# A graph-network kernel: the edges in eight parts in place of seven, the last part smaller and packed three tiles to two blocks

## The chip, the cores and the metric

One core of one Trainium2 chip runs one program. The metric is the device time of an execution in microseconds (us). A core has five engines that run their own instruction streams in order and wait for each other through semaphores: TensorE (PE; its weight loads are listed apart as PEld), VectorE (DVE), ScalarE (ACT), GpSimd (POOL) and SyncE (SP, which here only issues DMAs).

## The reference, cut to what matters

There are 6250 nodes and 100000 edges with 128 features each; the edges are sorted by `dst`.

```python
row, col = src, dst
h   = concat([x[row], x[col], edge_attr]) @ W + b      # 384 -> 128, one row per edge
h   = layernorm(h) * gamma + beta
msg = relu(h)
out = segment_sum(msg, row, 6250)                       # summed by source node
x   = layernorm(x + out)
```

## The kernel before

The edges come as 782 tiles of 128, sorted by destination, and the sum goes by source. So the kernel sorts the edges by source on the way. Source nodes are cut into 50 **blocks** of 125 nodes, and two neighbouring blocks make a **pair**, 25 pairs in all. The edges are cut into seven **splits** (table `SPLITS`: tiles in the split, tiles of room for each block, rows of a block that are always filled, and sizes of the pieces in which places are computed).

*The loop over pieces.* A piece `q` is four tiles, 196 pieces in all. For each, PE multiplies the edge features with their part of `W` (L620) and adds the destination's part by a one-hot matmul (L624, 126 of 128 rows used); DVE builds that one-hot (L608, `ohd`); ACT evicts the result to one of nine buffers `hs` (L634); and POOL scatters each tile's rows, one indirect DMA a tile (L651), to `sorted_d[s]` in DRAM, where every pair of blocks has its own region. The rows of the pair's two blocks alternate there. A scatter is tied by a semaphore to PE's progress in the same piece (`scatters`), and an eviction waits until the scatters of the buffer's earlier content are done. DVE, PE and ACT also compute the places (`places`).

*Old pairs.* When a split's scatters are done, its pairs can be worked off (class `Pairs`). A pair is loaded back (`load_pairs`, `hl`), a tile of 128 rows at a time: one-hots of the source nodes `ohe` (DVE, L749), their transposes (PE L761, ACT L765), a copy of the rows to PSUM (ACT L771), the source part added by three bf16 matmuls a tile (`pick`, PE L788), squares and their root (ACT L797, L800), the scaled and cut message (DVE L806, L812), the sum over edges by an f32 one-hot matmul (`sums`, PE L821, into the bank `pa`) and the addition to `acc` (DVE L827). Two pairs of four tiles go as one item of eight (a *twin*), where the code says so; the rest are single items. An item takes four steps, written in the table `FLOW`; `steps_due(q)` says how many steps must stand in the program by piece `q`. It is a straight line between marks: the pairs of split `s - 1` begin at the piece in which split `s` begins plus `LAG` = 5, and those of the last split but one must be over at piece 197.

*The tail.* The last split's pairs are worked off behind the last scatter (class `Unit`, function `tail`): a unit of one pair, eleven of two, and two of one. A unit does what `Pairs` does (loads L848, one-hots L855, transposes L865, copy to ACT or by an f32 identity matmul on PE L877, picks L888, squares L899, messages L914, sums L928, addition L934) and then the final layer norm (L941 to L984, partly on POOL). PE, DVE, ACT and SP run in the order in which the code is written.

*Names in the views.* `sel`, `hp`, `pa`, `tr` and `beside` are PSUM banks. L552 is a check, run once: a matmul with a single column of weights (`ones_f`).

## Time and profile before

| | us |
|---|---|
| three runs: median, lowest, highest | 1112.56, 1111.35, 1113.34 |
| the profiled execution, its own time | 1110.36 |
| its span, first to last instruction | 1108.6 |

| engine | PE | PEld | DVE | ACT | POOL |
|---|---|---|---|---|---|
| busy, us of the span | 865.3 | 799.1 | 858.5 | 767.3 | 796.4 |

A row of a timeline gives an instruction's start, its duration, engine, line, operation and tiles, and in brackets how long the engine sat idle before it and what ended that. A row that merges several ("x8") gives the stretch that they took. An instruction's duration reaches beyond the start of the next, since they are pipelined; what an instruction costs its engine is read from start to start. A row of windows gives a stretch and the busy time and count (x) of an engine in it.

### The profile page before, as it was taken

How to read it: one execution, taken by the hardware profiler on the slowest of the kernel's cores; microseconds unless marked ns; L12 is line 12 of the kernel's file. 1: busy time of each engine (PE TensorE's matmuls, PEld its weight loads, DVE VectorE, ACT ScalarE, POOL GpSimd, SP SyncE). 2: the span in 40 equal slices, each digit the busy share in tenths (PEclk: the TensorE clock that was granted, in tenths of full speed). 3: DMA queues.
4: the chain of work that ended last, by engine and by line, in shares of the span. 5: the costliest groups of instructions: out<-in, count | busy, mean ns of one | idle time of the engine just before them, and what ended most of it. 6: DMA issues, size and time to landing. Idle time of an engine off the chain costs nothing. (4 is left out here: it accounts for less than half of the span.)

```text
span 1108.6 us, 27458 instructions
## 1 busy us (share of the span) xinstructions
PE 865.3 (78%) x8878; PEld 799.1 (72%) x8878; DVE 858.5 (77%) x2436; ACT 767.3 (69%) x3049; POOL 796.4 (72%) x830
## 2 busy tenths in 40 slices
PE   6758656456989898698868868788889788885994
PEld 4647545446889788688768868678888788875773
DVE  8874656636898997869687777889898977764997
ACT  4324422126889888588676778798889787976896
POOL 2777777777777777777777777777777777775254
PEclk9878887668999999889899989999999999998998
DMA  6899999648877888777587767686789777833341
GB/s 212 246 279 270 278 316 296 217 161 273 285 249 233 256 250 261 240 222 226 165 263 235 250 196 237 210 291 204 223 250 292 239 215 210 245 115 117 117 132 64
DMA packets 132851, 250.59 MB, mean 226 GB/s; under 512 B 47805, under 2 KB 62031, under 8 KB 132697
## 3 DMA queue, kind: packets, MB, share of 16 engines
q1 hardware_dynamic: 106724, 195.30, 59.0%
q0 software_dynamic: 25104, 53.05, 13.4%
q8 instruction: 71, 1.16, 0.5%
q14 instruction: 82, 0.67, 0.2%
q10 hardware_dynamic: 870, 0.40, 0.1%
HBM read 155.49 MB, written 93.18 MB: 224 GB/s over the span
## 5 line engine op out<-in xcount | busy, mean ns | idle before, releaser
L651 POOL DMA_INDIRECT sorted<-hs,place_i x782 | 758.1, 969 | 243.3 <-issue 96.6
L821 PE MATMUL pa<-msg,ohe 128*128 128x130 f32 x1700 | 237.1, 288 | 30.8 <-DVE acc L827 22.8
L788 PE MATMUL sel<-xa,ohn 128*128 128x128 bf16 x2550 | 190.9, 224 | 83.2 <-ACT sel L771 82.5
L620 PEld LDWEIGHTS hp<-w,eT 128*128 128x128 f32 x1564 | 216.7, 213 | 49.8 <-issue 29.2
L620 PE MATMUL hp<-w,eT 128*128 128x128 f32 x1564 | 238.5, 301 | 16.7 <-ACT hs L634 16.7
L797 ACT ACTIVATE sq<-sel 128x128 f32<-128x128 f32 x850 | 224.0, 279 | 39.2 <-PE sel L788 37.7
L812 DVE SCALAR_TENSOR_TENSOR msg<-sel,rstd,cut 128x128 f32<-128x128 f32 x850 | 243.0, 345 | 8.8
L821 PEld LDWEIGHTS pa<-msg,ohe 128*128 128x128 f32 x1700 | 211.0, 197 | 38.9 <-DVE acc L827 26.2
L788 PEld LDWEIGHTS <-ohn 128*128 128x128 bf16 x2550 | 165.0, 100 | 93.8 <-issue 85.4
L797 ACT ACTIVATION_READ_ACCUMULATOR sq<-sel 128x1 f32 x850 | 178.8, 210 | 0.0
L749 DVE TENSOR_TENSOR ohe<-hl,beside 128x768 f32<-128x768 f32 (+2 forms) x130 | 132.2, 1017 | 36.8 <-PE beside L503 21.3
L634 ACT COPY hs<-hp 128x512 f32<-128x512 f32 x196 | 113.1, 579 | 50.3 <-PE hp L624 47.6
L771 ACT COPY sel<-hl 128x384 f32<-128x384 f32 (+1 forms) x250 | 132.1, 529 | 19.9 <-DVE msg L812 19.2
L765 ACT COPY ohn<-tr 128x768 bf16<-128x768 bf16 (+2 forms) x130 | 109.6, 843 | 5.9 <-PE tr L761 5.9
L608 DVE TENSOR_SCALAR ohd<-db,part_w 128x512 bf16<-128x512 bf16 x192 | 69.6, 363 | 56.5 <-DMA db<-drel_d 31.0
L827 DVE TENSOR_TENSOR acc<-acc,pa 128x260 f32<-128x260 f32 x150 | 62.8, 419 | 51.9 <-PE pa L821 51.6
L569 ACT COPY hs<-sloc 128x12 f32<-128x12 f32 x66 | 14.1, 214 | 112.6 <-DMA sorted<-hs,place_i 110.8
L624 PE MATMUL hp<-win,ohd 126*128 126x128 bf16 x782 | 81.7, 230 | 1.7 <-DMA win<-xb_d 1.7
L761 PE MATMUL tr<-ident_h,ohe 128*128 128x128 bf16 x850 | 70.8, 223 | 13.3 <-issue 10.4
L800 ACT ACTIVATE std<-ss,eps 128x3 f32<-128x3 f32 (+1 forms) x250 | 74.2, 297 | 8.1
L806 DVE RECIPROCAL rstd<-std 128x3 f32<-128x3 f32 (+1 forms) x250 | 42.3, 169 | 46.7 <-ACT std L800 44.5
L624 PEld LDWEIGHTS <-ohd 126*128 126x128 bf16 x782 | 65.8, 104 | 5.4 <-issue 2.0
(200 smaller groups left out, 1033.0 us busy)
## 6 DMA issues: line engine op xcount, KB each, us to landing
eT<-in_eT SPq DMA_DIRECT2D x96, 512.0 KB
hl<-sorted SPq DMA_DIRECT2D x75, 396.0 KB
db<-drel_d SPq DMA_DIRECT2D x96, 256.0 KB
sorted<-empty SPq DMA_DIRECT2D x100, 198.0 KB
hl<-sorted SPq DMA_DIRECT2D x75, 264.0 KB
hl<-sorted SPq DMA_DIRECT2D x25, 528.0 KB
sorted<-hs,place_i POOLq DMA_INDIRECT x782
sorted<-empty SPq DMA_DIRECT2D x75, 132.0 KB
```

Source lines behind the costliest of these rows:

```text
L620: pe(nc.tensor.matmul(hp[:, j, :], eT[:, at], w[:, 2, :], start=j == 0, stop=False, skip_group_check=True), 4)
L624: pe(nc.tensor.matmul(hp[:, j, :], oh[:3 * WN, at], win[:3 * WN, :], start=False, stop=j == m - 1, skip_group_check=True))
L634: nc.scalar.copy(hs[:, :m, 0:D], hp[:, :m, :])
L651: i = nc.gpsimd.indirect_dma_start(out=sorted_d[s][:, :], out_offset=bass.IndirectOffsetOnAxis(ap=place_i[:parts, t:t + 1], axis=0), in_=h ...
L749: nc.vector.tensor_tensor(self.ohe[:, :k, :], self.hl[:, :k, D:D + 1].to_broadcast([P, k, P]), row_bc(iota_p, k), op=ALU.is_equal)
L765: nc.scalar.copy(self.ohn[:, :self.k, :], self.tr[:, :self.k, :])
L771: nc.scalar.copy(self.sel[g][:, :m, :], self.hl[:, j0:j0 + m, 0:D])
L788: pe(nc.tensor.matmul(sel[:, j, :], self.ohn[:, j0 + j, :], xa[:, b, i * D:(i + 1) * D], start=False, stop=j == m - 1 and i == 2, skip_gro ...
L797: nc.scalar.activation(sq[:, j, :], self.sel[g][:, j, :], AF.Square, accum_out=ss[:, j:j + 1])
L800: nc.scalar.activation(std[:, :m], ss[:, :m], AF.Sqrt, bias=eps, scale=1.0 / D)
L812: nc.vector.scalar_tensor_tensor(self.msg[:, j0 + j, 0:D], self.sel[g][:, j, :], rstd[:, j:j + 1], cut, op0=ALU.mult, op1=ALU.max)
L821: pe(nc.tensor.matmul(self.pa[:, h, :], self.ohe[:, i * k + j, :], self.msg[:, i * k + j, :], start=(j == h), stop=(j == k - 2 + h)), 4)
```

## The change

The table has eight splits: the first and two of 124 tiles stand as before, then three of 80, one of 68, and the last of 58 tiles with 1.5 tiles of room for each block. So a pair of the last split has three tiles: one for each block, and a third whose first 64 rows belong to the first block and whose last 64 to the second (`shares`). The third tile is loaded by two DMAs of 64 partitions; in `pick` and `sums` each of its halves gets matmuls of its own, with 64 columns (L905) or 64 rows (L946) of weights. The sums of a unit go to two banks by block and not by pair, and two additions follow with a stride over the pairs. Old pairs are 900 tiles where they were 850, the tail's pairs 75 tiles where they were 100. The first one-hot of the tail is written two steps later among the old pairs' steps.

```diff
-          (124, 3, 192, [42, 42, 40]),
           (80, 2, 128, [40, 40]),
           (80, 2, 128, [40, 40]),
-          (82, 2, 128, [42, 40])]
+          (80, 2, 128, [40, 40]),
+          (68, 2, 128, [34, 34]),
+          (58, 1.5, 96, [30, 28])]
...
+def pair_rows(s):
+    return int(2 * SPLITS[s][1]) * P
+
+def shares(kp, j):
+    if j % 2 == 0 and j == kp - 1:
+        return [(h, slice(h * P // 2, (h + 1) * P // 2)) for h in range(2)]
+    return [(j % 2, slice(0, P))]
...
+    def load_rows(s, p, rows):
+        k, at = pair_rows(s) // P, p * pair_rows(s) * ROW
+        m = k // 2 * 2
+        nc.sync.dma_start(flat(rows[:, :m, :]),
+                          dram_ap(sorted_d[s], at, [[m * ROW, P], [1, m * ROW]]))
+        if m < k:
+            for h, c in shares(k, m):
+                nc.sync.dma_start(rows[c, m, :],
+                                  dram_ap(sorted_d[s], at + (m * P + h) * ROW,
+                                          [[2 * ROW, P // 2], [1, ROW]]))
...
     class Unit:
...
             for j in range(m):
-                b = 2 * (self.p0 + g) + j % 2
-                for i in range(3):
-                    nc.tensor.matmul(sel[:, j, :], self.ohn[:, j0 + j, :],
-                                     xa[:, b, i * D:(i + 1) * D], start=False,
-                                     stop=j == m - 1 and i == 2, skip_group_check=True)
+                for h, c in shares(m, j):
+                    for i in range(3):
+                        nc.tensor.matmul(sel[c, j, :], self.ohn[:, j0 + j, c],
+                                         xa[:, 2 * (self.p0 + g) + h, i * D:(i + 1) * D],
+                                         start=False, stop=j == m - 1 and i == 2,
+                                         skip_group_check=True)
...
         def sums(self, g):
-            if (self.p0 + g) % 2:
-                pa_t = psum.tile([P, PT, P], F32, name="hp", bufs=BANKS["hp"])
-                pa = flat(pa_t)
-            else:
-                pa = psum.tile([P, 512], F32, name="pa")
-            pa = pa[:, :2 * ACW].rearrange("p (h d) -> p h d", h=2)
+            if g == 0:
+                one = psum.tile([P, 512], F32, name="pa")
+                two = flat(psum.tile([P, PT, P], F32, name="hp", bufs=BANKS["hp"]))
+                self.pa = [t[:, :self.n * ACW].rearrange("p (g d) -> p g d", g=self.n)
+                           for t in (one, two)]
             for h in range(2):
-                for j in range(h, self.kp, 2):
+                parts = [(j, c) for j in range(self.kp) for i, c in shares(self.kp, j) if i == h]
+                for j, c in parts:
                     jj = g * self.kp + j
-                    nc.tensor.matmul(pa[:, h, :], self.ohe[:, jj, :], self.msg[:, jj, :],
-                                     start=(j == h), stop=(j == self.kp - 2 + h))
-            self.pa = {**getattr(self, "pa", {}), g: pa}
+                    nc.tensor.matmul(self.pa[h][:, g, :], self.ohe[c, jj, :], self.msg[c, jj, :],
+                                     start=(j == h), stop=(j == parts[-1][0]))
...
     work(n_tail - n_steps)
     for i in range(3):
         units[i].load()
-    work(1)
+    work(3)
     units[0].ones()
...
     units[0].square()
-    work(5)
+    work(n_tail + 11 - n_steps)
```

Three places show how the order moves. The first is DVE between the destination one-hots (`ohd`) of pieces 189 and 190, late in the loop. Before:

```order
L608 TENSOR_SCALAR ohd<-db,part_w 128x512
L749 TENSOR_TENSOR ohe<-hl,beside 128x1024
L806 RECIPROCAL rstd<-std 128x4
L812 SCALAR_TENSOR_TENSOR msg_2205<-sel,rstd,cut 128x128 x4
L827 TENSOR_TENSOR acc<-acc,pa 128x260
L608 TENSOR_SCALAR ohd<-db,part_w 128x512
```

The same place in the changed kernel (its lines are L619, L766, L824, L830, L846):

```order
L619 TENSOR_SCALAR ohd<-db,part_w 128x512
L846 TENSOR_TENSOR acc<-acc,pa 128x260
L824 RECIPROCAL rstd<-std 128x4
L830 SCALAR_TENSOR_TENSOR msg_2209<-sel,rstd,cut 128x128 x4
L766 TENSOR_TENSOR ohe<-hl,beside 128x1024
L824 RECIPROCAL rstd<-std 128x4
L830 SCALAR_TENSOR_TENSOR msg_2208<-sel,rstd,cut 128x128 x4
L846 TENSOR_TENSOR acc<-acc,pa 128x260 x2
L824 RECIPROCAL rstd<-std 128x4
L830 SCALAR_TENSOR_TENSOR msg_2208<-sel,rstd,cut 128x128 x4
L619 TENSOR_SCALAR ohd<-db,part_w 128x512
```

Three message groups of old pairs stand between the two pieces where one stood.

The second place is DVE where the tail begins; L855 (changed: L872) is the first one-hot of the tail, which needs rows of the last split. Before:

```order
L812 SCALAR_TENSOR_TENSOR msg_2205<-sel,rstd,cut 128x128 x4
L855 TENSOR_TENSOR ohe<-hl,beside 128x512
L827 TENSOR_TENSOR acc<-acc,pa 128x260
L806 RECIPROCAL rstd<-std 128x4
L812 SCALAR_TENSOR_TENSOR msg_2204<-sel,rstd,cut 128x128 x4
L855 TENSOR_TENSOR ohe<-hl,beside 128x1024
L827 TENSOR_TENSOR acc<-acc,pa 128x260
L806 RECIPROCAL rstd<-std 128x4
L812 SCALAR_TENSOR_TENSOR msg_2205<-sel,rstd,cut 128x128 x4
L827 TENSOR_TENSOR acc<-acc,pa 128x260
L855 TENSOR_TENSOR ohe<-hl,beside 128x1024
```

In the changed kernel:

```order
L830 SCALAR_TENSOR_TENSOR msg_2209<-sel,rstd,cut 128x128 x4
L872 TENSOR_TENSOR ohe<-hl,beside 128x384
L846 TENSOR_TENSOR acc<-acc,pa 128x260
L824 RECIPROCAL rstd<-std 128x4
L830 SCALAR_TENSOR_TENSOR msg_2208<-sel,rstd,cut 128x128 x4
L872 TENSOR_TENSOR ohe<-hl,beside 128x768
L846 TENSOR_TENSOR acc<-acc,pa 128x260
L872 TENSOR_TENSOR ohe<-hl,beside 128x768
```

Behind the tail's first one-hot stand three additions and two message groups of old pairs before, two and one now.

The third place is PE inside the tail, where the sums of a unit end and the next unit's copy and picks begin. Before, after the transposes:

```order
L865 MATMUL tr<-ident_h,ohe 128x128
L928 MATMUL hp<-msg_2204,ohe 128x130 x4
L928 MATMUL pa<-msg_2204,ohe 128x130 x4
L877 MATMUL hp<-hl,ident 128x512
L888 LDWEIGHTS ohn
L888 MATMUL hp<-xa,ohn 128x128
```

In the changed kernel (of each "x2" the second matmul has 64 rows of weights):

```order
L882 MATMUL tr<-ident_h,ohe 128x128
L946 MATMUL pa<-msg_2209,ohe 128x130 x2
L946 MATMUL hp<-msg_2209,ohe 128x130 x2
L946 MATMUL pa<-msg_2209,ohe 128x130 x2
L946 MATMUL hp<-msg_2209,ohe 128x130 x2
L894 MATMUL hp<-hl,ident 128x384
L905 LDWEIGHTS ohn
L905 MATMUL hp<-xa,ohn 128x128
```

As many matmuls stand there as before, eight, in an order of banks that alternates by block, and the copy is 384 wide in place of 512.

More of the change, by code (lines that the diff above doesn't have):

```diff
@@ L679, in open_late @@
             nc.tensor.matmul(flat(sel), ones_h, row_bc(ones_h, PT), start=True, stop=True)
-    KMAX = 2 * max(k for _, k, _, _ in SPLITS)
+    KMAX = int(2 * max(k for _, k, _, _ in SPLITS))
     MS = 2
@@ L785, in pick @@
             for j in range(m):
-                b = self.block(j0 + j)
-                for i in range(3):
-                    pe(nc.tensor.matmul(sel[:, j, :], self.ohn[:, j0 + j, :],
-                                        xa[:, b, i * D:(i + 1) * D], start=False,
-                                        stop=j == m - 1 and i == 2, skip_group_check=True))
+                p, jj = self.p + (j0 + j) // self.kp, (j0 + j) % self.kp
+                for h, c in shares(self.kp, jj):
+                    for i in range(3):
+                        pe(nc.tensor.matmul(sel[c, j, :], self.ohn[:, j0 + j, c],
+                                            xa[:, 2 * p + h, i * D:(i + 1) * D], start=False,
+                                            stop=j == m - 1 and i == 2, skip_group_check=True))
         def square(self, g):
@@ L819, in sums @@
             for h in range(2):
-                for j in range(h, k, 2):
-                    pe(nc.tensor.matmul(self.pa[:, h, :], self.ohe[:, i * k + j, :],
-                                        self.msg[:, i * k + j, :],
-                                        start=(j == h), stop=(j == k - 2 + h)), 4)
+                parts = [(j, c) for j in range(k) for g, c in shares(k, j) if g == h]
+                for j, c in parts:
+                    pe(nc.tensor.matmul(self.pa[:, h, :], self.ohe[c, i * k + j, :],
+                                        self.msg[c, i * k + j, :],
+                                        start=(j == h), stop=(j == parts[-1][0])), 4)
         def add(self, i=0):
@@ L1241, in tail @@
                 u(-1).sums(g)
-                u(-1).add(g)
+            for h in range(2):
+                u(-1).add(h)
             u(-1).begin(nc.gpsimd)
```

41 lines of the change are left out of this document (18 added, 23 removed).

## Prediction

> **What bounds the kernel now.** I read the page's slices and groups first, then POOL, then the last 100 us engine by engine.
>
> ```profile
> POOL 2777777777777777777777777777777777775254
> ```
> ```profile
> L651 POOL DMA_INDIRECT sorted<-hs,place_i x782 | 758.1, 969 | 243.3 <-issue 96.6
> ```
>
> POOL is equally busy from the second slice to the 36th: 782 scatters of 969 ns with 243.3 us of gaps between them, so one each 1.28 us and 1001 us in all, without a longer stop. Up to the last scatter POOL sets the time. DVE shows what follows it:
>
> ```profile
> 1012.75 1.13 DVE L812 SCALAR_TENSOR_TENSOR msg<-sel,rstd,cut 128x128 f32<-128x128 f32 x4
> 1022.11 0.69 DVE L855 TENSOR_TENSOR ohe<-hl,beside 128x512 f32<-128x512 f32 x1 [8.23 <-DMA hl<-sorted]
> 1022.72 0.42 DVE L827 TENSOR_TENSOR acc<-acc,pa 128x260 f32<-128x260 f32 x1
> 1023.05 0.17 DVE L806 RECIPROCAL rstd<-std 128x4 f32<-128x4 f32 x1
> 1023.25 1.13 DVE L812 SCALAR_TENSOR_TENSOR msg<-sel,rstd,cut 128x128 f32<-128x128 f32 x4
> ```
> ```profile
> 1017.30 0.87 POOL L651 DMA_INDIRECT sorted<-hs,place_i  x1 [0.30 <-issue]
> ```
>
> The old pairs' work is written up to 1014, then DVE sits 8.23 us until rows of the last split are back: the last scatter ends at 1018.2, and its rows are in SBUF 3.9 us later. Then the tail of 100 tiles runs. In its middle a unit of two pairs (eight tiles) looks so:
>
> ```profile
> 1057.07:1062.55 5.48, 5.48 (x56) 4.18 (x53) 5.41 (x24) 5.21 (x29) 3.26 (x4) 1.00 0.45 148
> ```
> ```profile
> 1057.07 1.11 PE L928 MATMUL hp<-msg,ohe 128*128 128x130 f32 x8
> 1058.02 1.06 PE L928 MATMUL pa<-msg,ohe 128*128 128x130 f32 x8
> 1058.91 1.02 PE L877 MATMUL sel<-hl,ident 128*128 128x512 f32 x2
> 1059.84 0.84 PE L888 MATMUL sel<-xa,ohn 128*128 128x128 bf16 x12
> 1060.52 1.08 PE L877 MATMUL sel<-hl,ident 128*128 128x512 f32 x2
> 1061.43 0.83 PE L888 MATMUL sel<-xa,ohn 128*128 128x128 bf16 x12
> 1062.10 0.61 PE L865 MATMUL tr<-ident_h,ohe 128*128 128x128 bf16 x8
> 1062.55 1.11 PE L928 MATMUL hp<-msg,ohe 128*128 128x130 f32 x8
> ```
> ```profile
> 1055.73 2.16 DVE L914 SCALAR_TENSOR_TENSOR msg<-sel,rstd,cut 128x128 f32<-128x128 f32 x8
> 1057.80 1.21 DVE L855 TENSOR_TENSOR ohe<-hl,beside 128x1024 f32<-128x1024 f32 x1
> 1058.93 0.42 DVE L934 TENSOR_TENSOR acc<-acc,hp 128x260 f32<-128x260 f32 x1
> ```
>
> In the window row the columns are PE, PEld, DVE, ACT and POOL: 5.48, 5.41 and 5.21 us of 5.48. Three engines are full at once, so the tail gets shorter only if all three do.
>
> **The change, part by part.** *A tail of 75 tiles.* DVE loses two of eight messages, 2 x 0.26 (1055.73 to 1057.80 is 2.07 for eight), and a quarter of its one-hot, 0.28 of 1.13: 5.41 becomes 4.61. The strided additions read as many elements and stay. ACT loses two squares and a quarter of a copy; its 5.21 falls too. On PE, start to start, sums are now 1.84 (1057.07 to 1058.91), the two copies 0.93 and 0.91, the picks 0.68 and 0.67, the transposes 0.45. Copies and transposes shrink by a quarter, to 1.38 and 0.34. The picks stay at twelve matmuls a pair and the sums at four f32 ones, since each half of the shared tile has its own: 1.35 and 1.84. PE by counts alone is 4.91.
>
> *What a half costs PE.* Before, all matmuls of the tail use the whole array. Now PE leaves that shape three times a pair: once in the picks (64 columns), twice in the sums (64 rows). Two places of the trace bound the price. The first is the end of the loop's step with and without L552, whose weights have one column:
>
> ```profile
> 909.29 0.61 PE L761 MATMUL tr<-ident_h,ohe 128*128 128x128 bf16 x8
> 909.74 1.11 PE L620 MATMUL hp<-w,eT 128*128 128x128 f32 x8
> 910.69 0.39 PE L624 MATMUL hp<-win,ohd 126*128 126x128 bf16 x4
> 910.91 0.83 PE L788 MATMUL sel<-xa,ohn 128*128 128x128 bf16 x12
> ```
> ```profile
> 915.19 0.61 PE L761 MATMUL tr<-ident_h,ohe 128*128 128x128 bf16 x8
> 915.73 0.19 PE L552 MATMUL beside<-bad,ones_f 128*1 128x6 f32 x2
> 915.86 1.16 PE L620 MATMUL hp<-w,eT 128*128 128x128 f32 x8
> 916.85 0.33 PE L624 MATMUL hp<-win,ohd 126*128 126x128 bf16 x3
> ```
>
> From the transposes to L624 it is 1.40 without and 1.66 with it: two instructions of six elements cost 0.26. PE stands before them (0.54 where the transposes take 0.45) and behind them; no semaphore is named there. The second place is L624 itself: 126 of 128 rows, four in 0.22, in stream at the pace of the full ones. So a detour costs nothing if a half is as good as 126 rows, and 0.26 if it is like one column. The upper end is 0.37, since L552 loads one column only, and a full f32 load may come on top: about the pitch of an f32 matmul, 0.11 to 0.12 (1057.07 to 1058.02 for eight). I take 0.26, the row that differs in kind as a half does. Six detours a unit are 1.56: PE needs 6.47, and the unit goes from 5.48 to 6.47 with PE alone as its bound. Over the eleven units of two pairs that is **+10.9 us**. The three single units are chains of waits in which three quarters of the work and the detours about cancel; I count nothing. Ends: -6.3 (detour free: 4.91) and +15.7 (0.37 for the sums).
>
> The Trainium skill, page "TensorEngine Tiling (Array Packing)", section "Tiling Modes", says that changing the tiling mode, unlike changing the tile within one, drains the engine; the pause before L552 agrees, and by this rule both halves of one pick share one drain. The same section says that tiles of one mode work in parallel. No row shows that; by it the 3 x 0.056 us of one half of each pick would hide behind the other's, an estimate of 4 us off over 25 pairs.
>
> *Old pairs of 900 tiles.* The middle of the loop has a store of slack. Scatters, then evictions (four tiles each), done by four times:
>
> ```profile
> 0.00:551.00 551.00, 402.86 (x415) 0.88 0.80 248
> 0.00:706.00 706.00, 520.66 (x537) 0.90 0.79 245
> 0.00:832.00 832.00, 616.46 (x636) 0.91 0.79 243
> 0.00:921.00 921.00, 684.12 (x706) 0.91 0.79 243
> ```
> ```profile
> 0.00:551.00 551.00, 63.53 (x110) 0.88 0.80 248
> 0.00:706.00 706.00, 81.26 (x141) 0.90 0.79 245
> 0.00:832.00 832.00, 93.07 (x161) 0.91 0.79 243
> 0.00:921.00 921.00, 104.31 (x181) 0.91 0.79 243
> ```
>
> ACT is ahead of POOL by 440 - 415 = 25 tiles, by 27 at piece 140, by 8 at piece 160, by 18 at piece 180. Between 140 and 160 the marks ask for 150 tiles of old pairs (7.5 a piece), and PE, DVE and ACT fall 19 tiles behind POOL's pace without POOL ever stopping; at 5 a piece they win ten back. In the change the 150 tiles stand between pieces 109 and 129: 25 - 19 leaves 6, two fewer than the 8 that sufficed. I count **+1 us** (0 to 4). Then come 40 pieces at 5 a piece, enough to fill the store again. Behind piece 186 the marks ask for 64 tiles in six pieces (10.7 a piece), then 36 in five. What this takes is measured on the same 100 tiles of the split before last:
>
> ```profile
> 934.50:975.30 40.80, 8.72 (x64) 7.79 (x64) 1.00 0.72 215
> 975.30:1012.60 37.30, 5.29 (x36) 4.71 (x36) 0.95 0.35 106
> ```
>
> These are L620, eight to a piece: 100 old tiles and 12.5 pieces took 78.1 us, counted from the first item's transposes to the last's. In the change about 9.5 pieces lie among them; a piece is 1.17 us on PE (909.74 to 910.91), so 74.6 us, or less where the steps stand denser. They can start when the 724th tile is scattered, 58 x 1.28 us before 1018.2, at 944; rows back and transposed some 6 us later (3.9 as above, then one-hot and waits), 950. The last transposes then run at about 1024, and the tail's first one-hot stands five steps behind them: 1025 to 1028, against 1022.1. The evictions lose some 20 of 27 tiles of lead here, so the last scatter should stay at 1018. The rows of the tail come later as well: SP takes 0.44 us for a load,
>
> ```profile
> 1052.60 0.88 SPq L848 DMA_DIRECT2D hl<-sorted  x2
> ```
>
> and a pair needs three: two more before the first unit is +0.9, six more before the second +2.6. Both fit into the time that the old pairs take. In the unit's period SP's 6 x 0.44 is hidden.
>
> *The one-hot two steps later.* One message group, its reciprocal and one addition (0.33 + 0.20 + 1.1 = 1.6 us of DVE, 1022.72 to 1024.4) leave the tail's beginning for the 8.23 us that DVE waited. If the old pairs now end at 1025, this wait is gone, and the step only changes order. Together the start is +4 - 1.6, **+2 us** (-1 to +8). The 25 more clears and one more set of places lie beside POOL in the loop, where PE, DVE and ACT have the store above.
>
> **Sum.** 1110.4 (the profiled execution: span 1108.6 and 1.8 around it) + 10.9 + 1 + 2 = 1124.3. The median of the runs is 2.2 above that execution, so **1126.5 us** for a median.
>
> **Rivals.** *Halves cost nothing extra* (faster). Then PE is 4.91 a unit, DVE 4.61, and the tail gains 6.3 us and about 1.5 more in its chains at both ends: 1110.4 - 7.8 + 3 + 2.2 = 1107.8. For it: L624 runs in stream, and a half has no fewer elements to stream. Against it: the pause around L552, a matmul without waits. The change gains from a detour below some 0.06 us (4.8 / 75) on, the other terms as above; near that lies no change. *The old pairs are late.* If the 100 tiles do not get faster than one message group in 2.9 us plus the pieces, or the store runs dry around piece 129 or 195 and POOL stops, the tail starts 8 to 10 us late on top of the longer units: 1133. For it: three engines with 65 of 78 us on PE in that stretch. Against it: 8.23 us of wait to fill. *The step does not do what it says*: the old pairs would stand sooner in the program but not on the clock, the rival before this one without its price; it is in the +2.
>
> **Chances.** Units bound by PE through detours 0.60 (1118 to 1133), halves free 0.24 (1104 to 1112), old pairs late 0.16 (1128 to 1140). A measurement can tell about 0.2%, 2.2 us, from no change. Faster takes most of the free halves, 0.2; the same 0.07; slower 0.73. The range 1106 to 1137 leaves some 0.1 out at each end.
>
> **What would show it.** In the middle of the tail the unit's period (sums to sums on PE): 6.5 if the forecast holds, 4.9 if halves are free. Gaps of about 0.1 us between the starts of matmuls at each change between full and half, without a semaphore. DVE and ACT then wait for PE, about 1.5 us a unit. DVE's wait before its first tail one-hot: short or gone. POOL's gaps still 0.3 us around 600 and 1000 us. The forecast is wrong if the period stays below 5.5, or if the last scatter moves by more than 4 us.

## The result, and the profile after

| | kernel before | changed kernel |
|---|---|---|
| median of 5 runs each, us | 1113.34 | 1159.66 |
| lowest, highest, us | 1111.35, 1114.04 | 1156.46, 1160.23 |
| ratio, 95% interval | | 1.0415, 1.0403 to 1.0427 |
| profiled execution: span, us | 1108.6 | 1157.9 |

The changed kernel is 46 us slower where some 14 were forecast, and above the range of 1106 to 1137 us. The span of the profiled execution grew by 49.3 us. Where, the slices of POOL and two timeline rows tell (POOL's last scatter, DVE's first tail one-hot).

```profile
POOL 3777777777777777777777777777776677532344
L662 POOL DMA_INDIRECT sorted<-hs,place_i x782 | 759.3, 971 | 275.2 <-issue 106.7
```
```profile
1050.37 0.87 POOL L662 DMA_INDIRECT sorted<-hs,place_i  x1 [0.31 <-issue]
```
```profile
1061.31 0.54 DVE L872 TENSOR_TENSOR ohe<-hl,beside 128x384 f32<-128x384 f32 x1
```

The scatters take the same 759 us, but POOL's gaps grew from 243.3 to 275.2 us: its slices are no longer even from the 31st on, at some 870 us. The last scatter ends at 1051.2 instead of 1018.2: **33 us** of the 49. The tail begins 10.1 us behind it, where it began 3.9 us behind. From the last scatter to the end are 106.7 us where there were 90.4: the other **16**.

**The loop.** Scatters, then evictions (four tiles each), done by four times, as in the prediction. The lead is the number of tiles that ACT has evicted and POOL has not yet scattered:

```profile
0.00:551.00 551.00, 402.98 (x415) 0.89 0.80 247
0.00:706.00 706.00, 520.82 (x537) 0.91 0.80 247
0.00:832.00 832.00, 616.15 (x635) 0.91 0.79 244
0.00:921.00 921.00, 677.67 (x698) 0.91 0.78 241
```
```profile
0.00:551.00 551.00, 63.76 (x110) 0.89 0.80 247
0.00:706.00 706.00, 79.96 (x138) 0.91 0.80 247
0.00:832.00 832.00, 93.25 (x161) 0.91 0.79 244
0.00:921.00 921.00, 101.93 (x176) 0.91 0.78 241
```

Four times the second less the first: ACT is ahead of POOL by 25, 15, 9 and 6 tiles, where it was 25, 27, 8 and 18. The scatters still keep to the old count at 706 (537) and 832 (635 for 636), so up to there the store paid. But in the 40 pieces that were to fill it again it does not fill, and at 921 POOL is eight scatters late. At 980 it is still eight late, first the changed kernel, then the kernel before:

```profile
0.00:980.00 980.00, 722.58 (x744) 0.91 0.78 240
0.00:980.00 980.00, 729.09 (x752) 0.92 0.78 241
```

At 1.28 us a scatter some 10 of the 33 us are lost by then. The other 23 are lost behind it, where the marks ask for 10.7 old tiles a piece and the lead is 8 tiles where it was 16 (188 and 192 evictions). POOL's timeline has the same split: from 90 us on it has eleven stops of 0.5 us or more between 802 and 911 us, 18 from 987 us on, and in the kernel before none. What the engines wait for, in all (us, times, longest), after and then before:

```profile
DVE acc L846 <- PE pa L840: 79.0, 65, 4.2
PE pa L840 <- DVE acc L846: 65.0, 40, 4.2
POOL sorted L662 <- PE pa L840: 37.0, 77, 2.9
```
```profile
DVE acc L827 <- PE pa L821: 51.6, 41, 3.7
PE pa L821 <- DVE acc L827: 22.8, 19, 2.4
```

PE's sums and DVE's additions wait for each other. One such place late in the loop, on PE, DVE and POOL:

```profile
995.51 1.11 PE L840 MATMUL pa<-msg,ohe 128*128 128x130 f32 x8
997.95 1.16 PE L840 MATMUL pa<-msg,ohe 128*128 128x130 f32 x8 [1.33 <-DVE acc L846]
998.94 0.83 PE L806 MATMUL sel<-xa,ohn 128*128 128x128 bf16 x12
999.61 0.61 PE L778 MATMUL tr<-ident_h,ohe 128*128 128x128 bf16 x8
1000.06 1.11 PE L631 MATMUL hp<-w,eT 128*128 128x128 f32 x8
```
```profile
996.44 1.13 DVE L830 SCALAR_TENSOR_TENSOR msg<-sel,rstd,cut 128x128 f32<-128x128 f32 x4
997.48 0.41 DVE L846 TENSOR_TENSOR acc<-acc,pa 128x260 f32<-128x260 f32 x1
```
```profile
999.16 0.97 POOL L662 DMA_INDIRECT sorted<-hs,place_i  x1 [2.25 <-PE pa L840]
```

A twin has two pairs, and both sums go to the one bank `pa`. The first pair's sums are issued from 995.51 on. The second pair's must wait until DVE has added the first. That addition stands behind a message group on DVE (996.44), so PE stops for 1.33 us, and behind it stand picks, transposes and the next eviction's matmuls (1000.06). POOL, tied to PE's progress, stops for 2.25 us. The twins are 44 (three times 12 and 8) where they were 20 (12 and 8): on the mean 1.14 us of PE's wait a twin before, 1.48 after.

The longest of these waits lie earlier, in the 40 pieces that were to fill the store:

```profile
758.29 1.92 DVE L467 TENSOR_TENSOR_SCAN sc<-oh,beside 128x850 f16<-128x850 bf16 x1
761.35 0.41 DVE L846 TENSOR_TENSOR acc<-acc,pa 128x260 f32<-128x260 f32 x1
761.82 2.10 PE L840 MATMUL pa<-msg,ohe 128*128 128x130 f32 x8 [4.20 <-DVE acc L846]
```

L467 belongs to `places`: DVE computes places for a later split, then a message group, and only then the addition, and PE stands for 4.20 us. In each of the seven longest waits of these 40 pieces (2.7 us and more, between 674 and 881 us) DVE does a part of `places` ahead of the addition.

**The tail.** A unit of two pairs on all engines (the columns as before), and its PE:

```profile
1097.99:1104.58 6.59, 6.59 (x53) 4.51 (x51) 4.79 (x21) 4.48 (x25) 3.25 (x4) 1.00 0.39 106
```
```profile
1091.39 0.86 PE L946 MATMUL pa<-msg,ohe 128*128 128x130 f32 x4
1092.18 0.91 PE L946 MATMUL hp<-msg,ohe 128*128 128x130 f32 x4
1093.02 0.91 PE L946 MATMUL pa<-msg,ohe 128*128 128x130 f32 x4
1093.86 0.91 PE L946 MATMUL hp<-msg,ohe 128*128 128x130 f32 x4
1094.69 0.91 PE L894 MATMUL hp<-hl,ident 128*128 128x384 f32 x2
1095.44 0.79 PE L905 MATMUL hp<-xa,ohn 128*128 128x128 bf16 x12
1096.16 0.91 PE L894 MATMUL sel<-hl,ident 128*128 128x384 f32 x2
```

The period is 6.59 us, forecast 6.47; PE alone is full, DVE and ACT are busy for 4.79 and 4.48. A detour is, as in the prediction, one departure of PE from the whole array and back. The price is not spread over the detours as the forecast spread it. Four instructions of sums, one whole tile and one half, take 0.79 to 0.84 us from start to start, 0.825 on the mean of the four (1091.39 to 1094.69); four of eight took 0.95 / 2 = 0.475 before. A detour in the sums costs 0.35, not 0.26. A pair's picks, 1095.44 to 1096.16, take 0.72 where they took 0.67: a detour in the picks costs about 0.05.

### The profile page after: what moved, and what is told of

It is laid out like the page before. It is cut to its first block, busy times and chain, and to the rows that moved or that the text cites. A ratio compares the mean times of both kernels' runs of the same rounds, so it can differ in the third digit from the quotient of the medians.

```text
span 1157.9 us, 28370 instructions
## 1 busy us (share of the span) xinstructions
PE 913.1 (79%) x9179; PEld 836.5 (72%) x9179; DVE 883.8 (76%) x2515; ACT 783.9 (68%) x3102; POOL 797.6 (69%) x830
## 5 line engine op out<-in xcount | busy, mean ns | idle before, releaser
L662 POOL DMA_INDIRECT sorted<-hs,place_i x782 | 759.3, 971 | 275.2 <-issue 106.7
L840 PE MATMUL pa<-msg,ohe 128*128 128x130 f32 x1800 | 257.9, 292 | 71.4 <-DVE acc L846 65.0
L840 PEld LDWEIGHTS pa<-msg,ohe 128*128 128x128 f32 x1800 | 227.3, 199 | 82.8 <-DVE acc L846 72.4
L815 ACT ACTIVATE sq<-sel 128x128 f32<-128x128 f32 x900 | 237.7, 281 | 72.4 <-PE sel L806 72.2
L830 DVE SCALAR_TENSOR_TENSOR msg<-sel,rstd,cut 128x128 f32<-128x128 f32 x900 | 255.8, 345 | 8.8
L806 PE MATMUL sel<-xa,ohn 128*128 128x128 bf16 x2700 | 202.5, 226 | 55.5 <-ACT sel L788 54.3
L766 DVE TENSOR_TENSOR ohe<-hl,beside 128x1024 f32<-128x1024 f32 (+2 forms) x131 | 138.9, 1060 | 29.4 <-PE beside L514 15.4
L788 ACT COPY sel<-hl 128x512 f32<-128x512 f32 (+1 forms) x250 | 137.3, 550 | 18.4 <-DVE msg L830 17.0
L846 DVE TENSOR_TENSOR acc<-acc,pa 128x260 f32<-128x260 f32 x175 | 73.3, 419 | 80.3 <-PE pa L840 79.0
L782 ACT COPY ohn<-tr 128x1024 bf16<-128x1024 bf16 (+2 forms) x131 | 115.2, 879 | 16.9 <-PE tr L778 16.9
L619 DVE TENSOR_SCALAR ohd<-db,part_w 128x512 bf16<-128x512 bf16 x192 | 70.4, 367 | 60.5 <-DMA db<-drel_d 38.7
L818 ACT ACTIVATE std<-ss,eps 128x4 f32<-128x4 f32 (+1 forms) x250 | 74.3, 297 | 8.1
L778 PEld LDWEIGHTS <-ohe 128*128 128x128 bf16 x900 | 60.2, 103 | 12.4 <-issue 10.4
```

Of the source, the lines that this page charges most:

```text
L662: i = nc.gpsimd.indirect_dma_start(out=sorted_d[s][:, :], out_offset=bass.IndirectOffsetOnAxis(ap=place_i[:parts, t:t + 1], axis=0), in_=h ...
L766: nc.vector.tensor_tensor(self.ohe[:, :k, :], self.hl[:, :k, D:D + 1].to_broadcast([P, k, P]), row_bc(iota_p, k), op=ALU.is_equal)
L778: pe(nc.tensor.transpose(tr[:, j, :], half[:, j0 + j, 1::2], ident_h))
L782: nc.scalar.copy(self.ohn[:, :self.k, :], self.tr[:, :self.k, :])
L788: nc.scalar.copy(self.sel[g][:, :m, :], self.hl[:, j0:j0 + m, 0:D])
L806: pe(nc.tensor.matmul(sel[c, j, :], self.ohn[:, j0 + j, c], xa[:, 2 * p + h, i * D:(i + 1) * D], start=False, stop=j == m - 1 and i == 2, ...
```

## The experiments

Each time stands beside runs of the kernel before on the same chip. Five chips were used. On two of them (e5 to e8, and e9 to e12) every program took 22 to 23% longer, the kernel before too (1354.5 and 1370.2 us), with POOL's gaps about doubled; the cause stays open. From these two only comparisons on the same chip are read, and PE in the tail, which keeps its pace there: a unit takes 6.59 us in e6 as in the changed kernel, and 5.48 in e5 as in the kernel before.

### Loop or tail: no shared tile (e1)

```diff
-          (58, 1.5, 96, [30, 28])]
+          (58, 2, 96, [30, 28])]
```

> The changed kernel with room for two whole tiles a block in its last split (58 tiles, four tiles a pair, none shared): the tail has 100 tiles again and no half matmul, all else as changed. Theory A (two separate losses: the loop's old pairs stop POOL and move the last scatter by 33 us; in the tail the halves lengthen the unit): the last scatter stays at 1051 (within 5), the unit of two pairs goes from 6.59 back to 5.4 to 5.6, the time is 1145 to 1149. Rival (the tail's units are long for another reason, such as the two banks by block or the strided additions): the unit stays above 6.2 and the time above 1154. Rival (the shared tile also slows the loop): the last scatter comes back below 1040.

Measured: 1147.35 us, with before at 1111.87 (ratio 1.0307, 1.0287 to 1.0328). The last scatter, and a unit of the tail on all engines:

```profile
1051.51 0.87 POOL L662 DMA_INDIRECT sorted<-hs,place_i  x1 [0.30 <-issue]
```
```profile
1097.57:1103.04 5.47, 5.47 (x55) 4.18 (x53) 5.40 (x24) 5.20 (x29) 3.25 (x4) 1.00 0.47 151
```

The loop's loss stays whole, the unit is 5.47 us again: two separate losses, and the shared tile makes only the smaller one. The two banks by block and the strided additions, which stay in this kernel, cost the period nothing.

### The one-hot two steps later, alone (e3)

```diff
-    work(1)
+    work(3)
     units[0].ones()
...
-    work(5)
+    work(n_tail + 11 - n_steps)
```

> The kernel before with one edit: the first one-hot of the tail stands two steps later among the steps of the last old pairs. All theories: it only changes the order in a stretch where DVE waits 8 us; 1111 to 1114 against 1112.6 before. A rival that puts part of the 49 us on this step would need 1115 or more.

Measured: 1111.18 us, ratio 0.9993 (0.9983 to 1.0002): no change, as all expected.

### How many twins, or how many tiles (e2)

```diff
-          (80, 2, 128, [40, 40]),
-          (80, 2, 128, [40, 40]),
-          (80, 2, 128, [40, 40]),
-          (68, 2, 128, [34, 34]),
+          (124, 3, 192, [42, 42, 40]),
+          (124, 3, 192, [42, 42, 40]),
+          (60, 2, 96, [30, 30]),
```

> The changed kernel with another table, of the same 900 old tiles and 75 tiles of tail: splits of 168, four times 124, 60 and 58 tiles with room for 4, 3, 3, 3, 3, 2 and 1.5 tiles a block. Only the 60 tiles before the last split go by twins, instead of four splits. Theory A1 (the number of old tiles eats the lead of the evictions; how they are grouped does not matter): the last scatter stays at 1045 to 1055, the time at 1152 to 1160. Theory A2 (the twins' two sums that share one bank, each waiting for the other's addition, hold PE up): about three quarters of the waits of the sums for the addition go (65 us to below 30) and the last scatter comes back to 1018 to 1030, the time to 1125 to 1137.

Measured: 1161.33 us, ratio 1.0455 (1.0437 to 1.0472). Neither theory had it. The waits of the sums fell to 10.4 us, as A2 said; the last scatter still ended at 1047.2, as A1 said. The reason is another place: with only 60 tiles in the split before the last, 150 old tiles stand between the marks at pieces 171 and 186, ten a piece. The engines in that stretch (PE, PEld, DVE, ACT, POOL of 40 us):

```profile
930.00:970.00 40.00, 35.53 (x425) 33.54 (x425) 33.06 (x105) 39.09 (x175) 24.86 (x26) 1.00 0.66 208
```

ACT is full, 39.09 of 40 us, and POOL does 26 scatters where it does 32 otherwise. PE's sums wait for no addition in these 40 us. So a stretch dense enough stops POOL by load alone, without any wait for a bank. In the changed kernel ACT is busy for 36.77 us of the same stretch. This table was a bad test for the question, since it moved the density too; the next runs leave the table alone.

### The sums apart, and a second bank (e4, e6, e9, e10, e13)

The mutual wait is taken away in the changed kernel in two ways, with the table as it is. First by time: a twin's second sums and second addition stand a step later, single sums two steps, so that the uses of `pa` stand two steps apart (e4).

```diff
-    FLOW = [(15, twin(lambda x: x.add(1))), (14, twin(lambda x: x.add(0))),
+    FLOW = [(16, twin(lambda x: x.add(1))), (14, twin(lambda x: x.add(0))),
...
-            (13, twin(lambda x: x.sums(0))), (14, twin(lambda x: x.sums(1))),
+            (13, twin(lambda x: x.sums(0))), (15, twin(lambda x: x.sums(1))),
...
-            (10, single(lambda x: x.sums())),
+            (12, single(lambda x: x.sums())),
```

> The changed kernel with the twins' second sums one step later, second addition one step later, and the sums of single old pairs two steps later, so that the uses of the one bank of sums stand two steps apart. Theory A1 (the load of old tiles stops POOL): no change, last scatter 1047 to 1053, time 1155 to 1160. Theory A2 (the shared bank of sums holds PE up): the waits of the sums for the addition fall from 65 us to below 25, the last scatter comes back to 1018 to 1035, the time to 1125 to 1143.

Measured: 1125.29 us with before at 1111.87, ratio 1.0127 (1.0111 to 1.0144). Its last scatter, the wait of the sums, and scatters and evictions done by the four times:

```profile
1017.58 0.87 POOL L662 DMA_INDIRECT sorted<-hs,place_i  x1 [0.30 <-issue]
```
```profile
PE pa L840 <- DVE acc L846: 23.6, 21, 2.8
```
```profile
0.00:832.00 832.00, 616.45 (x636) 0.90 0.80 249
0.00:921.00 921.00, 684.11 (x706) 0.91 0.80 248
```
```profile
0.00:832.00 832.00, 95.55 (x165) 0.90 0.80 249
0.00:921.00 921.00, 105.91 (x183) 0.91 0.80 248
```

The last scatter is back at 1018.4, all 33 us. The lead is 24 tiles at 832 and 26 at 921 (9 and 6 in the changed kernel): at five old tiles a piece the store is filled again, with the same 900 tiles. The load theory A1 falls for this table, though the load has its price: between 921 and 1000 us the lead falls from 26 to 8. In e4 the lead pays it, and POOL makes no stop of 0.5 us from 90 us on.

Then by space: all steps stay, the second sums go to a bank of the pool `hp` (e6, e9 and e13 are this kernel on three chips).

```diff
-            pa_t = psum.tile([P, 512], F32, name="pa")
+            if i:
+                pa_t = flat(psum.tile([P, PT, P], F32, name="hp", bufs=BANKS["hp"]))
+            else:
+                pa_t = psum.tile([P, 512], F32, name="pa")
```

> The changed kernel with all steps where they were, but the twins' second sums go to a bank of the evictions' pool instead of the bank of the first sums, so that they no longer wait for the first addition. Theory A2 (the one bank of sums is what cost the loop 33 us): waits of the sums for the addition below 30 us, last scatter 1018 to 1030, time 1125 to 1137. Rival (the spread run gained by standing its single sums or its additions elsewhere, not by the bank): last scatter above 1040, time above 1147. Rival (the bank of the evictions is now what is waited for): in between, with evictions on PE waiting for additions.

> The same kernel as the run with the second bank (all steps where the changed kernel has them, the twins' second sums in a bank of the evictions' pool), on another chip: on the first one every program, the kernel before too, took 22% longer with POOL's gaps doubled, so that the loop's loss could not be read there. Theory A2 (the one bank of sums is what cost the loop 33 us): waits of the sums for the addition below 30 us, last scatter 1018 to 1030, time 1125 to 1137. Rival (the spread run gained by standing its single sums or its additions elsewhere): last scatter above 1040, time above 1147. Rival (the evictions now wait for the bank in place of the sums): last scatter between 1030 and 1045.

And the third of e4's numbers alone, the single sums two steps later (e10):

```diff
-            (10, single(lambda x: x.sums())),
+            (12, single(lambda x: x.sums())),
```

> The changed kernel with one of the three numbers of the spread run alone: the sums of single old pairs stand two steps later, the twins' sums and additions where the changed kernel has them. Theory A2 (what holds PE up is that a twin's second sums wait for its first addition): the waits stay above 50 us, the last scatter at 1042 to 1052, the time at 1150 to 1160. Rival (the single sums carried the gain): 1125 to 1137.

e6, e9 and e10 ran on the two chips named above, so the times that were expected can't be held against them. e6 took 1368.90 us with before at 1354.5 (ratio 1.0104, 1.0073 to 1.0135), and its sums wait 4.4 us for the addition. On the other chip e9 and e10 part: the last scatter ends at 1269.8 with the second bank and at 1294.9 with the singles alone, and the times are 1383.81 and 1412.11 with before at 1370.16 (ratios 1.0122, 1.0079 to 1.0164, and 1.0316, 1.0280 to 1.0353). The singles alone do not mend it: with them the sums still wait 49.5 us. Then the second bank on a chip where before takes 1111.35:

> The kernel with the second bank once more, for a chip on which the kernel before takes 1112 us. Theory A2 (the one bank of sums cost the loop 33 us): last scatter 1018 to 1030, time 1125 to 1140 (its tail started late on the other chips, by up to 10 us). Rival (the additions' places in the spread run carried part of it): last scatter above 1035.

Measured: 1126.41 us, ratio 1.0128 (1.0110 to 1.0146).

```profile
1021.08 0.87 POOL L662 DMA_INDIRECT sorted<-hs,place_i  x1 [0.31 <-issue]
```
```profile
PE pa L843 <- DVE acc L849: 5.9, 6, 2.4
```

The last scatter ends at 1021.95, so 29 of the 33 us are back. Two edits that have nothing in common but the bank give nearly the same, 1125.3 and 1126.4: it is shown that the loop's loss hangs on the wait for the bank. One thing goes along with it. In the windows 680 to 785 and 785 to 897 us the granted TensorE clock is 0.93 and 0.89 in the changed kernel, and 0.98 and 0.94 in e4 and in e13. It came back with the bank and no edit moved it alone, so its share is not separated.

### The same edit before (e5, e12, e15)

e4's three numbers in the kernel before, on three chips.

> The kernel before with the same edit of the sums' steps as the run of the changed kernel with spread sums (twins' second sums and addition a step later, single sums two steps later). Theory (the shared bank of sums costs time only where it runs the lead of the evictions down to nothing; before, POOL never stopped for it): the sums' waits for the addition fall from 22.8 us to below 12, the last scatter stays at 1016 to 1019, the time at 1109.5 to 1113. Rival (the spread sums are simply a better order everywhere): 1108 or less.

> The kernel before with the spread sums, on another chip (see the run with the second bank). Theory (the shared bank costs time only where it runs the lead of the evictions down to nothing; before, POOL never stopped for it): waits of the sums for the addition below 15 us instead of 22.8, last scatter 1016 to 1019, time 1109.5 to 1113. Rival (the spread sums are a better order everywhere): 1108 or less.

> The kernel before with the spread sums, once more for a chip on which the kernel before takes 1112 us. Theory: waits of the sums for the addition below 15 us, last scatter 1016 to 1019, time 1109.5 to 1113. Rival (the spread sums are a better order everywhere): 1108 or less.

Measured: 1347.78 us (ratio 0.9944, 0.9914 to 0.9974) and 1368.39 us (0.9990, 0.9964 to 1.0015) on the two chips that take longer, the first of them a gain of 0.6% that stays unexplained; on the third 1113.37 us, ratio 1.0022 (1.0013 to 1.0031), last scatter 1018.1, waits of the sums 9.3 us instead of 22.8. So on a chip where the kernel before takes some 1112 us, 13 us of such waits go and no time is gained (the median is 0.4 us above the expected range): before, POOL makes no stop of 0.5 us from 90 us on, and the waits lay beside its work.

### The price of the halves (e7, e8)

Both start from e4 (unit 6.59 us). e7 does both whole tiles of a pair first, then both halves:

```diff
-            for h in range(2):
-                parts = [(j, c) for j in range(self.kp) for i, c in shares(self.kp, j) if i == h]
-                for j, c in parts:
+            for j in range(self.kp):
+                for h, c in shares(self.kp, j):
                     jj = g * self.kp + j
...
-                                     start=(j == h), stop=(j == parts[-1][0]))
+                                     start=(j == h), stop=(j == self.kp - 1))
```

> The changed kernel with spread sums (1125.3) and one edit in the tail: for each pair first both whole tiles' sums, then the two row halves one behind the other, so that the sums leave the whole array twice a unit of two pairs and not four times. Theory T1 (the price is for the change of shape, 0.36 us each in the sums): the unit goes from 6.59 to 5.8 to 5.95 us, or 0.2 less if the two row halves run side by side; the time is 1115 to 1118. Rival T2 (each half matmul is slow by itself, wherever it stands): the unit stays at 6.4 to 6.6, the time at 1123 to 1126.

e8 keeps the order and takes all 128 rows. It leaves out the separation of the two blocks in the shared tile, so its sums are not those that the task asks for; it serves as a price only:

```diff
-                    nc.tensor.matmul(self.pa[h][:, g, :], self.ohe[c, jj, :], self.msg[c, jj, :],
+                    nc.tensor.matmul(self.pa[h][:, g, :], self.ohe[:, jj, :], self.msg[:, jj, :],
```

> The changed kernel with spread sums (1125.3), but the shared tile's sums use all 128 rows for both blocks, so that both blocks also receive the other one's messages of the last split; as many matmuls as before, no row halves. It prices the row halves alone. Theory T1: four changes of shape less, 0.36 us each, take 1.44 off the unit: 5.1 to 5.3 us; time 1108 to 1112. Rival T3 (the row halves are cheap, the column halves of the picks carry the price): unit 6.2 to 6.5, time 1121 to 1125.

Measured: units of 5.38 us (e7) and 5.03 us (e8); the times, 1362.14 and 1357.79 with before at 1354.5, are those of the first chip that takes longer. A pair's sums in e7, and a unit of e8:

```profile
1303.08 0.44 PE L945 MATMUL pa<-msg,ohe 128*128 128x130 f32 x2
1303.36 0.39 PE L945 MATMUL hp<-msg,ohe 128*128 128x130 f32 x2
1303.67 0.38 PE L945 MATMUL pa<-msg,ohe 64*128 64x130 f32 x1
1303.68 0.38 PE L945 MATMUL hp<-msg,ohe 64*128 64x130 f32 x1
1303.89 0.27 PE L945 MATMUL pa<-msg,ohe 64*128 64x130 f32 x1
1303.90 0.27 PE L945 MATMUL hp<-msg,ohe 64*128 64x130 f32 x1
1304.10 0.49 PE L945 MATMUL pa<-msg,ohe 128*128 128x130 f32 x2
1304.42 0.39 PE L945 MATMUL hp<-msg,ohe 128*128 128x130 f32 x2
```
```profile
1301.07:1306.10 5.03, 5.03 (x53) 3.92 (x51) 4.79 (x22) 4.47 (x24) 3.25 (x4) 1.00 0.49 132
```

Without row halves 1.56 us go, 0.39 for each of four: T2 and T3 fall, and the row halves carry nearly the whole price. Both units came out below the ranges of T1 (5.6 to 5.95 and 5.1 to 5.3). The six detours together are 6.59 - 4.91 = 1.68 us over the counts, of which 5.03 - 4.91 = 0.12 is left for the two in the picks. In e7 the lower and the upper half start 0.01 us apart (1303.67 and 1303.68, then 1303.89 and 1303.90): they run side by side, each with its own 64 rows of weights. So e7's 1.21 us are two detours (0.78) and four f32 instructions that run beside others (0.44 at 0.11 each). The price itself shows as four pauses, two at each change. The pace is 0.11 us an instruction. The last two whole ones take 0.31 (1303.36 to 1303.67), the first half 0.22, the way out 0.20 (1303.90 to 1304.10) and the next two whole ones 0.32 (1304.10 to 1304.42): 0.09 + 0.11 + 0.09 + 0.10 = 0.39 too much.

### A version ahead of both (e11, e14, e16, e17)

From e4, the first pair of a unit does its halves last and the second does its halves first, so that a unit's sums leave the whole array once (e11; these lines stand in place of the loops over `h` and `parts`):

```diff
+            js = range(self.kp) if g == 0 else [2, 0, 1]
+            own = [(j, h, c) for j in js for h, c in shares(self.kp, j)]
+            for j, h, c in own:
+                jj, mine = g * self.kp + j, [i for i, b, _ in own if b == h]
+                nc.tensor.matmul(self.pa[h][:, g, :], self.ohe[c, jj, :], self.msg[c, jj, :],
+                                 start=(j == mine[0]), stop=(j == mine[-1]))
```

> The changed kernel with spread sums and, in the tail, the row halves of the first pair of a unit last among its sums and those of the second pair first, so that a unit's sums leave the whole array once and not four times. From 6.59 us a unit with four and 5.38 with two changes (halves together), T1 gives 4.8 to 5.1 us a unit, with PE no longer alone at the bound; the time is 1106 to 1109 where the kernel before has 1111.9, a version ahead of both. Rival (DVE and ACT bound the unit below 5.3, or the start of the tail, 3 us later than before, eats it): 1111 to 1114, no gain.

Measured on the second chip that takes longer: the unit is 5.0 us; 1375.53 us with before at 1370.16, ratio 1.0038 (1.0014 to 1.0063). e14 also reads the shared tile by one DMA:

```diff
-            for h, c in shares(k, m):
-                nc.sync.dma_start(rows[c, m, :],
-                                  dram_ap(sorted_d[s], at + (m * P + h) * ROW,
-                                          [[2 * ROW, P // 2], [1, ROW]]))
+            nc.sync.dma_start(rows[:, m, :],
+                              dram_ap(sorted_d[s], at + m * P * ROW,
+                                      [[ROW, 2], [2 * ROW, P // 2], [1, ROW]]))
```

> The changed kernel with spread sums, one change of shape a unit in the tail's sums, and the shared tile read by one DMA and not by two. The unit is 5.0 us on PE. Theory (SP issues loads back to back at the start of the tail, 1.7 us a pair, and the first one-hots wait 3 us for rows): with two DMAs a pair these waits fall below 1 us; 1104 to 1107.5 where the kernel before has 1111.9. Rival (the rows are late for another reason than the number of loads): 1107 to 1110. Rival (no gain: the tail's other engines take its place): 1111 or more.

e16 is e14 with the shared tile of five units loaded by ACT (`load_rows` gets the queue as an argument):

```diff
-                load_rows(self.s, self.p0 + i, self.hl[:, j0:j0 + self.kp, :])
+                load_rows(self.s, self.p0 + i, self.hl[:, j0:j0 + self.kp, :],
+                          nc.scalar if 5 <= self.p0 < 15 else nc.sync)
```

> The best version so far (1109.7, with the kernel before at 1111.35), but the loads of the shared tile of units 3 to 7 are issued by ACT and not by SP. Theory (the loads are slow because one queue takes one at a time): the first one-hots' waits for rows fall from 5.9 us in all to below 3, the time to 1105 to 1108. Rival (the transfers themselves, in pieces of 528 and 1056 bytes, are the limit, whatever the queue; or ACT loses what the rows gain): 1108.5 or more.

e17 is e11's kernel on another chip.

> The version with one change of shape a unit and two loads for the shared tile, as in the changed kernel. If the number of loads were the limit: 2 to 4 us slower than with one, 1112 to 1114. If not, as the waits of the run with one load say (5.9 us against 3.3 with two and the longer unit): within 1.5 us of it, 1108 to 1111.

Measured: e14 1109.70 us, ratio 0.9985 (0.9976 to 0.9994); e16 1115.04 us, ratio 1.0033 (1.0023 to 1.0042); e17 1107.70 us with before at 1110.83, **ratio 0.9971 (0.9961 to 0.9982)**, the best: 0.3% ahead of the kernel before, though its interval overlaps with that of e14. e14's theory fell; that of e16 held for the waits and not for the time. The number of loads is not what the tail's start waits for: DVE's first one-hots wait 5.9 us for rows with one load (1.57, 0.80, 2.36, 0.72, 0.40) and 4.3 with two (0.62, 1.73, 1.93). e16 says little about queues: DVE no longer waits for rows, but the squares of the last old pairs on ACT lost 6.3 us to one wait that the profile puts down to a load. From one pair's loads to the next pass 2.0 to 2.3 us with one load for the shared tile (e14, 1024 to 1046 us) and 1.7 to 1.9 with two (e17, 1025 to 1037 us). What sets this time stays open.

## Why the prediction was wrong

**The bound, POOL up to the last scatter, then three engines: right** before, and the reason why the loop's loss counted in full.

**A tail of 75 tiles, +10.9 us: right in the bound, and in size by luck.** The period was 6.47 in the forecast and 6.59 in the trace, so 11 units cost 12.2 us, with PE alone as the bound; DVE's 4.61 was 4.79. e1 gives as much from the other side, 1159.66 - 1147.35 = 12.3 us, though its own runs lie 8 us apart. The detour's mean price is 1.68 / 6 = 0.28 where 0.26 was taken from the row with one column. But it was no one price. In the sums it lies at the upper end that the text gave (0.37 there, 0.35 to 0.39 here), in the picks near nothing (0.05 to 0.06). The two errors cancel, which no row before had promised. The sentence from the Trainium skill, page "TensorEngine Tiling (Array Packing)", section "Tiling Modes", that a change of the tiling mode drains the engine and that tiles of one mode work in parallel, agrees with e7: pauses of about 0.1 us at each change, and halves 0.01 us apart. The forecast named such gaps as a sign; there are two at each change. In the changed kernel's sums each half stood alone between whole tiles, so every half paid for its own change.

**The middle, +1 us: right in itself.** At 680 us, where the dense stretch ends, both kernels have done 516 scatters, and the changed one's lead is 8 tiles (131 evictions) where the forecast had 6. POOL went on, to 635 of 636 scatters at 832 us.

**The failed step: "Then come 40 pieces at 5 a piece, enough to fill the store again", and with it "the last scatter should stay at 1018".** It moved by 33 us. The rate of refilling was read from 20 pieces of the kernel before (160 to 180, evicted from 832 to 921 us) and carried over to 40 pieces (129 to 169) by the number of tiles alone. Both stretches hold 12 twins in 20 pieces. But in the old one PE's sums waited for the bank `pa` for 9.9 us, in six waits, and the lead grew by ten tiles all the same. In the changed kernel they waited for 13.7 us in the first 20 pieces (six waits, 674 to 770 us) and for 22.8 us in the next 20 (eleven, up to 881 us); the lead was 8 tiles at 680 us, 13 at 760 and 6 at 880. With the sums apart (e4) the waits were 8.6 and 4.6 us, and the lead 7, 15 and 22. So what the step took over was the rate that one length of these waits allows. It never asked how long they would be where the pairs now stand, nor that 44 twins make such waits where 20 did (22.8 us of them stood in the profile of before, in 19 places).

The trace shows what makes a wait longer there, 2.3 and 2.1 us on the mean where it was 1.65. In these pieces DVE still computes places, for 25.0 and 24.6 us of the two stretches against 16.8 of the old one, and in the longest waits such work stands ahead of the addition. No run moves the places alone, so this part is read from the trace and not tested. The forecast had put the places of the loop at nothing, beside POOL.

e4 and e13 show that the step's sum over tiles holds once the bank is free: 26 and 25 tiles of lead at 921. The next step, that the dense end takes some 20 of 27 tiles of lead and no time, holds in e4 as well (26 to 8 by 1000 us). In the changed kernel there was no such lead, and the same end took the larger part of the 33 us, some 23. With the refilling set right, the forecast of 1126.5 stands beside 1125.3 and 1126.4.

**The start of the tail, +2 us: too small.** The first one-hot stood 10.1 us behind the last scatter, 6.2 later than before. With the sums apart (e4) it stands 5.9 behind, 2.0 later, as forecast: the rest went with the wait for the bank. As forecast too, DVE in the changed kernel has no wait for rows ahead of it, and 0.58 us in e4. SP's loads cost more than the 0.44 us that the forecast took: 0.52 to 0.59 each, back to back, in e17.

**The rivals.** That halves cost nothing fell with the period. "The old pairs are late" named the right event, a store that runs dry with POOL stopping, and one of its two places, the end around piece 195, where most of the loss fell. It gave it 8 to 10 us and put it down to load alone. What emptied the store came between its two places, by a wait. Its price should have been worked out for all pieces left once the lead is gone, and not for one place.

## What to carry to other kernels

Where work is hidden behind another engine by a lead, count what each added item makes the engines wait for each other, and not only how long they are busy: a bank with one buffer between two engines costs nothing while the lead lasts, and time on the slowest engine from the moment it is gone. Ask of each wait that the profile lists and that costs nothing now how many there will be after the change, and what else its engines do at the place to which it moves. A rate read from one stretch holds for another only if the waits in it stay as long. Where parts of the array are used, put parts that fit beside each other one behind the other and change shape once.

## What the runs showed of the hardware

- Row halves of an f32 matmul (64 of 128 rows) between whole ones cost 0.35 to 0.39 us a detour; column halves of bf16 picks 0.05 to 0.06. That the price differs so much between the two was not expected. Each change into or out of the row halves shows two pauses of about 0.1 us over the pace of 0.11 us an instruction (e7).
- Two row halves that write to different banks start within 0.01 us of each other, and a unit's sums with all four halves in one stretch take the unit to 5.0 us, as fast as with all 128 rows in every sum (5.03).
- Two of the five chips took 22 to 23% longer for each of the eight runs on them and for the kernel before, with POOL's gaps doubled (476 to 521 us where 243 is usual) while PE in the tail kept its pace (6.59 us a unit in e6, 5.48 in e5): an edit that frees PE in the loop can read differently there (e5 0.9944, e15 1.0022).
